# Image-row ConvNeXt kernel: channel sums from PSUM, w1 centered by broadcast transposes, image 0 multiplied before its norm

## The chip, the cores and the metric

The kernel runs on one core of a Trainium2 chip. The metric is the device time of one execution in microseconds; the median of three runs is given. A core has TensorE (PE), VectorE (DVE), ScalarE (ACT), GpSimd (POOL) and the queue SP, which only issues DMAs. Each takes its instructions in order and waits on semaphores for the others.

## The reference

The input is 32 images of 384 channels and 28x28 points, float32. Layer 0 is a ConvNeXt block, layer 1 a gate (only the first concerns us here):

```python
y = conv(x, dw_w, 7x7, padding 3, one filter per channel) + dw_b
mu, var = mean and variance of y over the channels
y = (y - mu) * rsqrt(var + 1e-6) * ln_g + ln_b
y = gelu(y @ w1 + b1)                      # 384 -> 1536
gx = sqrt(sum over the points of y**2); nx = gx / (mean of gx over channels + 1e-6)
y = grn_g * (y * nx) + grn_b + y
x = x + (y @ w2 + b2)                      # 1536 -> 384
# layer 1: per image, mean/max/min of x over the points -> 384 logits; sigmoid(logit + x)
```

## The kernel before

It has two stages under one scheduler, which takes the program in the order it is written and moves an instruction ahead where it counts it as ready; `keep` (keep_in_program_order) pins the order of those it is given.

**Stage 1, convolution of all images.** 48 steps `s` of 8 channels (`TC`), four "pairs" each. In `conv`, a channel takes three matmuls (L639, L641, L643) with a band matrix `tmat` from DRAM as weights and `xt` as the moving side; rows are cut into 7 groups of 4 image rows (`NJ`), so 7 x 32 images = 224 columns. The result `pc` (PSUM, one bank for a pair, 4 banks) is turned by VectorE into `yt` (L646), squared by ScalarE (L651), and the squares of four channels are added to `ssum` by GpSimd (L663). `yt` goes to DRAM `yd` after each step, and `sums_y` (L669) reduces the step's 8 channels to the running channel sum, which is the ninth row of the next `yt`. Beside it, every four steps the next 32 channels of x are loaded, padded (`pad_x`, L452) and turned by TensorE (`turn_x`, L464; copied out of PSUM at L473 or L475).

Also in stage 1 the weights are prepared. w1 is loaded into `ws`; `center_w` forms b1 + w1'ln_b (`pb`, L545), multiplies w1 by ln_g (L551) and takes each column's mean over the channels away, by products with a matrix of -1/C (`pm`, L559, added at L564). With columns that sum to zero, the mean of y need not be taken away before the product. `form_w` makes sums of weight blocks (L530, L533, L536), which go to DRAM as `u1d` and `u2d`: stage 2 multiplies 3x2 and 4x4 blocks with fewer products than blocks, by sums of weight blocks (UPSTEPS, STEPS) and of data blocks (FORMS, SUMS). `U1` and `U2` are the steps at which these begin, `later` holds the step of each weight load.

The last two steps are computed twice, for images 0 to 15 and then 16 to 31, so that the norm of the first half is ready earlier. `finish` makes 1/sqrt(var + eps) of a half (L692 to L699) and stores it as `rsd`. `first_image` spreads the norm's row for image 0 over all partitions by TensorE (`pr`, L729), multiplies the rows of image 0 by it (L736) and makes its ten data forms (`forms_up`, L342) on VectorE.

**Stage 2, image by image.** `up(b)` (L913) does the first product, 15 steps for each of 4 groups of weight tiles, in two halves `t2` = 0 and 2; its PSUM results are copied by ScalarE (L920) or added by VectorE (L922 to L930) into `y`. `gelu` (L883) and `square` (L889) are ScalarE's, `grn` makes the scale of each channel, `scale` (L315, L317) applies it, `sums` (L1002) makes 39 data sums on GpSimd, `down(b)` (L1041) does the second product in 38 steps. `normed(b)` (L308) multiplies the rows of image b, loaded back from `yd`, by its norm `rb`, which comes by DMA from `rsd`; `forms_up(b)` follows on GpSimd. What is done beside the products is written out by hand: `within(b)` and `beside(b)` hang each piece on a step, `(t2, 2 * i + t - t2)` in `up` and `i` in `down`. For image 0, `within(0)` hangs normed(1) and forms_up(1) into `up(0)`, and `within(1)` hangs image 0's second half of gelus, its squares, `grn`, scales and sums into `up(1)`; `down(0)` comes after `up(1)`.

Memory of stage 1's pools (`tp`, `xtp`, `ufp`, `ycp`, `sqp`) is taken again by stage 2's, in order of address: weights, `rb`, `te`, `junk` and the first of `y` lie on `tp`, the rest of `y` and `xp` on `xtp`, `d_room` on the end of `xtp` and what follows it. A new pool's first writer waits until the old pools that it lies on are done with. Before the change the late sums and norms lie in a last `xt` tile (`late_tiles`).

Of the kernel before, what the change touches and what calls it, by code (L numbers as in the profile page):

```python
# [33 lines left out]
TC = 8  # L34
# [163 lines left out]
def convnext_gate_kernel(  # L198
# [75 lines left out]
    def load_y(b):  # L274
        yi = yis[b] = yip.tile([P, CB, NQD, YR], F32, tag="yi", name=f"yi_{b}")
        rb = rbs[b] = rbp.tile([P, NQD, YR], F32, tag="rb", name=f"rb_{b}")

        with tc.issue_after(last_u2[-1]) if last_u2 else ExitStack():
            for cb in range(CB):
                load_y_part(b, yi, cb, 0, P)  # L280
        base = rsd[0 if b < B0 else 1]
        nc.sync.dma_start(
            rb,
            bass.AP(
                tensor=base.tensor,
                offset=base.offset + b * YR,
                ap=[[0, P], [B * YR, NQD], [1, YR]],
            ),
        )
# [29 lines left out]
    def forms_up(b, eng=nc.gpsimd):  # L319

        acc = accs.pop(b)
# [13 lines left out]
        n = 0  # L335
        for name, place, in0, in1, op in FORMS:
            if place and name == "w":
                d = o[place]
            else:
                d = af[n]  # L340
                n += 1
            tc.keep_in_program_order(eng.tensor_tensor(d, o[in0], o[in1], op))  # L342
            o[name] = d


    with ExitStack() as one:
# [5 lines left out]
        psc = one.enter_context(tc.tile_pool(name="psc", bufs=4, space=bass.MemoryType.PSUM))  # L352
        sqp = one.enter_context(tc.tile_pool(name="sqp", bufs=2))

# [69 lines left out]
        ssum = tp.tile([P, SQ, YR], F32, name="ssum")  # L424
        dws = tp.tile([P, 1], F32, name="dws")
        less = tp.tile([P, P], F32, name="less")
        nc.vector.memset(less, -1.0 / C)
# [56 lines left out]
        U1, U2 = 6, 24  # L484
# [38 lines left out]
        def form_w(name, wv, text, dst):  # L523
# [8 lines left out]
            else:  # L532
                nc.gpsimd.tensor_scalar(t, blks[0][1], float(blks[0][0]), None, ALU.mult)  # L533
# [5 lines left out]
        def center_w(part):  # L539

            if part == 0:
                pb = psx.tile([P, 4, P], F32, tag="pt", name="pb").rearrange("p a b -> p (a b)")
                for f in range(FB):
                    for cb in range(CB):
                        nc.tensor.matmul(  # L545
                            pb[:, f : f + 1], w1r[:, cb, f * P : (f + 1) * P],
                            lnb_t[:, cb : cb + 1], start=(cb == 0), stop=(cb == CB - 1),
                        )
                nc.vector.tensor_tensor(b1f, pb[:, :FB], b1_t, ALU.add)
                for cb in range(CB):  # L550
                    nc.vector.tensor_scalar(  # L551
                        w1r[:, cb], w1r[:, cb], lng_t[:, cb : cb + 1], None, ALU.mult
                    )
                return
            f0 = (part - 1) * 4 * P
            pm = psx.tile([P, 4, P], F32, tag="pt", name=f"pm_{part}")
            pm = pm.rearrange("p a b -> p (a b)")
            for cb in range(CB):
                nc.tensor.matmul(  # L559
                    pm, less, w1r[:, cb, f0 : f0 + 4 * P], start=(cb == 0), stop=(cb == CB - 1)  # L560
                )
            for cb in range(CB):
                w = w1r[:, cb, f0 : f0 + 4 * P]
                nc.vector.tensor_tensor(w, w, pm, ALU.add)  # L564
# [12 lines left out]
        for i in range(NG):  # L577
# [20 lines left out]
            3: (  # L598
# [7 lines left out]
            1: (fv, fvec.rearrange("v (fb p) -> p v fb", p=P)),  # L606
            2: (cv, cvec.rearrange("v (cb p) -> p v cb", p=P)),
# [7 lines left out]
        def conv(s, c2, yt, xt, b0, b1):  # L615
# [30 lines left out]
            nc.vector.transpose(yt[:, cy : cy + 2, :], pc[:, :, :N])  # L646
            nonlocal sq
            if cy % SQ == 0:
                sq = sqp.tile([P, SQ, YR], F32, tag="sq", name=f"sq_{cc}_{b0}")
            for ci in range(2):  # L650
                nc.scalar.activation(  # L651
                    sq[:, cy % SQ + ci, :], yt[:, cy + ci, :], AF.Square,
                    bias=dwb[:, cc + ci : cc + ci + 1], scale=1.0,
                )
            if cy % SQ == SQ - 2:
                if cc < SQ:
                    nc.gpsimd.tensor_copy(ssum, sq)
                elif b1 < B:
                    nc.gpsimd.tensor_tensor(
                        late["s2"], ssum if s == NK - 2 and cy < SQ else late["s2"], sq, ALU.add  # L660
                    )
                else:
                    nc.gpsimd.tensor_tensor(ssum, ssum, sq, ALU.add)  # L663
# [3 lines left out]
        def sums_y(dst, yt, n0, n1):  # L667

            nc.vector.tensor_reduce(  # L669
                dst, yt[:, n0:n1, :].rearrange("p c n -> p n c"), AX.X, ALU.add  # L670
            )

        def new_yt(name):
            return ycp.tile([P, TC + 1, YR], F32, tag="yc", name=name)

        late, pcs = {}, []

        def late_tiles():

            t = new_xt(NX).rearrange("p c n -> p (c n)")  # L680
            n = 0
            for name, c in (
                ("yb0", TC + 1), ("yb1", TC + 1), ("s2", SQ), *((f"t{i}", 1) for i in range(10))
            ):
                late[name] = t[:, n * YR : (n + c) * YR].rearrange("p (c n) -> p c n", n=YR)
                n += c

        def finish(yt, part, s2, half):

            s1, s2r, mu, va = (late[f"t{1 + 5 * half + i}"][:, 0] for i in range(4))  # L690
            sums_y(s1, yt, TC - SQ, TC + 1)
            nc.vector.tensor_reduce(s2r, s2.rearrange("p c n -> p n c"), AX.X, ALU.add)  # L692
            nc.vector.scalar_tensor_tensor(mu, s1, dws, part, ALU.add, ALU.add)
            nc.vector.scalar_tensor_tensor(s1, mu, 1.0 / C**2, mu, ALU.mult, ALU.mult)
            nc.vector.scalar_tensor_tensor(va, s2r, 1.0 / C, s1, ALU.mult, ALU.subtract)
            nc.vector.tensor_scalar(va, va, 0.0, EPS, ALU.max, ALU.add)
            nc.scalar.activation(s2r, va, AF.Sqrt)
            rs = s1
            nc.vector.reciprocal(rs, s2r)  # L699
            nc.scalar.dma_start(rsd[half], rs)  # L700
            return rs
# [6 lines left out]
        def spread(k, q, xn):  # L708
            for n in plan[q]:
# [4 lines left out]
                turn_x(i, h, xn)  # L714

        def first_image(n, yt):

            if n == 1:
                firsts["rs"] = finish(yt, firsts["part"], late["s2"], 0)
            elif n == 2 * PAIRS:  # L720
                rs = firsts["rs"]
                pr = [
                    psx.tile([P, 4, P], F32, tag="pt", name=f"pr_{i}").rearrange(
                        "p a b -> p (a b)"
                    )[:, : 2 * YR].rearrange("p (q n) -> p q n", n=YR)
                    for i in range(2)
                ]
                for q in range(NQD):
                    nc.tensor.matmul(  # L729
                        pr[q // 2][:, q % 2], ident[:, q * B : q * B + 1].to_broadcast([P, P]),  # L730
                        rs, start=True, stop=True,
                    )
                accs[0] = room_acc
                for cb in (1, 2, 0):
                    for i in range(2):
                        nc.vector.scalar_tensor_tensor(  # L736
                            room_acc[:, cb, i * NH : (i + 1) * NH].rearrange(
                                "p (r w) -> p r w", w=HW
# [515 lines left out]
```

## Time and profile before

| | us |
|---|---|
| median of 3 runs | 3106.68 (3104.93 to 3108.34) |
| the profiled execution | 3105.7 |
| its span | 3103.9 |
| TensorE busy in the span | 3021.0 (97%) |
| VectorE, ScalarE, GpSimd busy | 2110.7, 1772.9, 2455.4 |

Stage 1 takes the first 541 us, the rest is stage 2, 32 images of which each later one takes the same steps. A matmul of float32 shows as two records in the trace, a transpose as one; 16 records of L639 are one convolution step.

### The profile page before, as it was taken

To read this page: it belongs to the slowest core of one execution; us is meant where nothing else is said; L and a number is where in the kernel's file an instruction comes from. 1 tells how busy PE (TensorE), PEld (TensorE's weight loads), DVE (VectorE), ACT (ScalarE), POOL (GpSimd) and SP (SyncE) were. 2 spreads that over 40 slices of the span, in tenths; PEclk is the share of its full clock that TensorE was granted. 3 is DMA by queue.
4 is the path that set the end of the run, shared out by engine and by line. 5 is a ranking of instruction groups with operands and counts; after the bars stand their busy time and mean duration, and the time that the engine had idled before them with its cause. 6 is when DMAs were issued, how large, how long until landed. Compare 5 with 4: busy or idle time off the path is not lost.

```text
span 3103.9 us, 43870 instructions
## 1 busy us (share of the span) xinstructions
PE 3021.0 (97%) x14437; PEld 2441.4 (79%) x14437; DVE 2110.7 (68%) x4502; ACT 1772.9 (57%) x2886; POOL 2455.4 (79%) x1841
## 2 busy tenths in 40 slices
PE   7999989699999999999999999999999999999998
PEld 7899989377777777777777777777777777777777
DVE  5688778766666666666666666666666666666666
ACT  4354443465666666666666666666666666666662
POOL 3365868279888888888888888888888888888897
PEclk9899999899999999999999999999999999999999
DMA  9799987555666666666666666666666666666646
GB/s 337 260 356 363 330 313 265 155 158 159 198 201 200 202 202 200 201 202 201 200 202 202 201 201 201 201 201 202 202 200 201 202 201 201 202 201 199 196 152 202
DMA packets 287946, 672.77 MB, mean 217 GB/s; under 512 B 31183, under 2 KB 111082, under 8 KB 281706
## 3 DMA queue, kind: packets, MB, share of 16 engines
q1 hardware_dynamic: 274340, 630.94, 61.8%
q10 hardware_dynamic: 13382, 39.03, 3.3%
q8 instruction: 118, 1.93, 0.3%
q14 instruction: 106, 0.87, 0.1%
HBM read 575.11 MB, written 94.76 MB: 216 GB/s over the span
## 4 chain that ended last, share of the span: by engine, by line
PE 86%; DVE 6%; POOL 4%; DMA 2%; issue 1%; ACT 1%; SPq 0%; DVEq 0%; ACTq 0%; POOLq 0%
PE ph_C L913 13%; PE ph_A L913 12%; PE ph_B L913 11%; PE pz_A L1041 8%; PE pz_C L1041 8%; PE pz_F L1041 7%; PE pz_D L1041 7%; PE pc L639 4%; PE pc L641 3%; PE pc L643 3%; PE pz_H L1041 2%; PE pt L464 2%; PE pz_I L1041 2%; PE pz_E L1041 2%; POOL d_room L1002 2%; DVE room L308 2%
## 5 line engine op out<-in xcount | busy, mean ns | idle before, releaser
L317 ACT ACTIVATE y<-y,fv,gsc 128x784 f32<-128x784 f32 x372 | 359.0, 1031 | 469.2 <-DVE gsc L949 469.2
L1002 POOL TENSOR_TENSOR d_room<-y 128x588 f32<-128x588 f32 x253 | 364.6, 1442 | 316.7 <-PE pz_B L1041 192.2
L913 PE MATMUL ph_B<-room,ws 128*128 128x392 f32 x1240 | 461.8, 495 | 12.7 <-ACT y L920 8.5
L913 PE MATMUL ph_C<-room,ws 128*128 128x392 f32 x1240 | 463.4, 496 | 5.2 <-DVE y L926 2.6
L883 ACT ACTIVATE y<-y,b1f 128x784 f32<-128x784 f32 x384 | 350.4, 945 | 206.7 <-DVE y L928 184.0
L913 PE MATMUL ph_A<-room,ws 128*128 128x392 f32 x1240 | 459.0, 492 | 3.0 <-POOL room L342 2.0
L1002 POOL TENSOR_TENSOR d_room<-d_room,y 128x588 f32<-128x588 f32 x308 | 440.8, 1436 | 16.8
L913 PEld LDWEIGHTS ph_C<-room,ws 128*128 128x128 f32 x1240 | 234.3, 191 | 188.9 <-DVE y L926 27.7
L913 PEld LDWEIGHTS ph_B<-room,ws 128*128 128x128 f32 x1240 | 235.8, 191 | 178.1 <-ACT y L920 9.5
L913 PEld LDWEIGHTS ph_A<-room,ws 128*128 128x128 f32 x1240 | 235.7, 190 | 176.3 <-POOL room L342 2.7
L889 ACT ACTIVATE junk<-y 128x784 f32<-128x784 f32 x384 | 329.2, 857 | 9.0
L663 POOL TENSOR_TENSOR ssum<-ssum,sq 128x896 f32<-128x896 f32 x95 | 198.8, 2093 | 167.5 <-ACT sq L651 165.0
L1002 POOL TENSOR_TENSOR d_room<-y,d_room 128x588 f32<-128x588 f32 x214 | 306.0, 1435 | 27.2 <-PE pz_D L1041 15.7
L342 POOL TENSOR_TENSOR room<-room 128x392 f32<-128x392 f32 x300 | 300.4, 1018 | 11.8
L1002 POOL TENSOR_TENSOR y<-y 128x588 f32<-128x588 f32 x180 | 258.7, 1437 | 7.1
L924 DVE TENSOR_TENSOR y<-y,ph_B 128x392 f32<-128x392 f32 x256 | 137.4, 556 | 158.9 <-ACT y L883 127.6
L651 ACT ACTIVATE sq<-yt,dwb 128x224 f32<-128x224 f32 x376 | 152.7, 470 | 158.9 <-DVE yt L646 149.0
L922 DVE TENSOR_TENSOR y<-y,ph_C 128x392 f32<-128x392 f32 x384 | 212.6, 561 | 26.9 <-PE ph_C L913 1.2
L639 PE MATMUL pc<-xt,tmat 128*128 128x224 f32 x736 | 202.9, 358 | 15.4 <-DVE yt L646 7.2
L1041 PE MATMUL pz_A<-d_room,u 128*128 128x196 f32 x1050 | 202.9, 329 | 0.4 <-DMA u<-u2d 0.3
L1041 PEld LDWEIGHTS pz_A<-d_room,u 128*128 128x128 f32 x1050 | 178.8, 190 | 8.1 <-issue 0.6
L641 PE MATMUL pc<-xt,tmat 128*96 128x192 f32 x736 | 181.2, 328 | 0.0
(267 smaller groups left out, 6400.2 us busy)
## 6 DMA issues: line engine op xcount, KB each, us to landing
u<-u2d SPq DMA_DIRECT2D x487, 384.0 KB, 3.7
ws<-u1d SPq DMA_DIRECT2D x384, 320.0 KB, 3.0
tmat<-fs SPq DMA_DIRECT2D x47, 1420.0 KB, 10.0
ws<-u2d SPq DMA_DIRECT2D x121, 384.0 KB, 4.1
yi<-yd SPq DMA_DIRECT2D x95, 448.0 KB, 6.2
yd<-yt SPq DMA_DIRECT2D x46, 896.0 KB, 5.8
x<-in_x SPq DMA_DIRECT2D x32, 1176.0 KB, 5.5
out<-x ACTq DMA_DIRECT2D x31, 1176.0 KB, 9.5
```

The costliest lines, as they stand in the source:

```text
L317: eng.activation(out, in_, AF.Identity, bias=add, scale=mul)
L342: tc.keep_in_program_order(eng.tensor_tensor(d, o[in0], o[in1], op))
L639: keep(nc.tensor.matmul(po, t[:, c, P : 2 * P], xc, start=True, stop=False))
L641: nc.tensor.matmul(lo, t[:, c, 2 * P : T0 + MW], after, start=False, stop=False)
L651: nc.scalar.activation(sq[:, cy % SQ + ci, :], yt[:, cy + ci, :], AF.Square, bias=dwb[:, cc + ci : cc + ci + 1], scale=1.0,)
L663: nc.gpsimd.tensor_tensor(ssum, ssum, sq, ALU.add)
L883: nc.scalar.activation(y, y, AF.Gelu, bias=b1f[:, f : f + 1], scale=1.0)
L889: nc.scalar.activation(junk, ys[b][:, f, :], AF.Square, accum_out=ssqs[b][:, f : f + 1])
L913: nc.tensor.matmul(banks[t, bk][:, :NH], wts[t][:, i % UG, :], o[opnd], start=(first == 1), stop=True, skip_group_check=True,)
L922: nc.vector.tensor_tensor(d, d, p, ALU.add)
L1002: nc.gpsimd.tensor_tensor(d[0], o[a][0], o[c][0], ALU.add if sign == "+" else ALU.subtract)
L1041: nc.tensor.matmul(pz[:, :NQ4], wt[:, i % UD, t, :], o[opnd][0][:, t, :], start=(first and t == 0), stop=(t == KD - 1), skip_group_check=True,
```

## The change

Five things are done.

1. *Channel sums straight from PSUM.* `sums_y` goes. VectorE adds each `pc` to an accumulator `acc` (two channels side by side) right after the transpose, and ScalarE squares `pc` itself instead of `yt`. Sums stay in the layout of `pc`; `finish` adds and reduces them, works on half of the columns and turns the result by one VectorE transpose. `ssum`, `acc`, `fin`, `dws` lie in a new pool `finp` at the end of stage 1's memory; `pc` has 5 banks instead of 4.
2. *Centering of w1 later.* w1 is loaded at step 2 instead of 3 and centered after steps 7 to 9 instead of 4 and 5 (`U1` 10 instead of 6, and three forms in two steps). `pb` takes two columns, ln_b and -ln_g/C, so that its second gives the means `mcol`; twelve products of a broadcast column of `mcol` with the identity spread them over the partitions, and one VectorE instruction multiplies by ln_g and adds.
3. *First terms of weight forms and half of `turn_x`'s copies* go to ScalarE.
4. *Image 0's products are made of its rows without the norm.* `first_image` adds only dw_b to the rows (`raw`), the first two blocks before the half steps, where q, t and u are formed on GpSimd; the other forms follow on VectorE after them, and only then both `finish`. Since the norm is a factor of each point, it is put on after the product: `stretch` multiplies y of image 0 by `rb` before each gelu.
5. `rb` of image 0 lies in `d_room`; normed(1) and forms_up(1) move from steps (0, 18) and (0, 24) to (0, 24) and (2, 0).

The diff, cut:

```diff
+    def load_rb(b):
+        if b == 0:
+            rb = d_room[:, : NQD * YR].rearrange("p (q n) -> p q n", n=YR)
+        else:
+            rb = rbp.tile([P, NQD, YR], F32, tag="rb", name=f"rb_{b}")
+        rbs[b] = rb
...
+        if b in feats:
+            o, af = feats[b], early_af.pop()
+            make_forms(b, eng, o, af, [d for d in FORMS if d[0] not in EARLY])
+            return
...
+        make_forms(b, eng, o, af, [d for d in FORMS if not early or d[0] in EARLY])
+    EARLY, early_af = ("q", "t", "u"), []
...
-        psc = one.enter_context(tc.tile_pool(name="psc", bufs=4, space=bass.MemoryType.PSUM))
+        psc = one.enter_context(tc.tile_pool(name="psc", bufs=5, space=bass.MemoryType.PSUM))
+        finp = one.enter_context(tc.tile_pool(name="finp", bufs=1))
...
-        ssum = tp.tile([P, SQ, YR], F32, name="ssum")
+        ssum = finp.tile([P, SQ, N], F32, name="ssum")
+        acc = finp.tile([P, 2, N], F32, name="acc")
+        fin = finp.tile([P, 3, N], F32, name="fin")
+        for t in (ssum, acc, fin[:, 0]):
+            nc.gpsimd.memset(t, 0.0)
...
-        U1, U2 = 6, 24
+        U1, U2 = 10, 23
...
-                nc.gpsimd.tensor_scalar(t, blks[0][1], float(blks[0][0]), None, ALU.mult)
+                nc.scalar.activation(t, blks[0][1], AF.Identity, scale=float(blks[0][0]))
...
+                nc.vector.tensor_copy(lr[:, :, 0], lnb_t)
+                nc.vector.tensor_scalar(lr[:, :, 1], lng_t, -1.0 / C, None, ALU.mult)
...
-                            pb[:, f : f + 1], w1r[:, cb, f * P : (f + 1) * P],
-                            lnb_t[:, cb : cb + 1], start=(cb == 0), stop=(cb == CB - 1),
+                            pb[:, 2 * f : 2 * f + 2], w1r[:, cb, f * P : (f + 1) * P],
+                            lr[:, cb], start=(cb == 0), stop=(cb == CB - 1),
...
+            for i in range(4):
+                nc.tensor.matmul(
+                    pm[:, i], mcol[:, f0 + i : f0 + i + 1].to_broadcast([P, P]), ident,
+                    start=True, stop=True,
+                )
             for cb in range(CB):
-                nc.tensor.matmul(
-                    pm, less, w1r[:, cb, f0 : f0 + 4 * P], start=(cb == 0), stop=(cb == CB - 1)
-                )
-            for cb in range(CB):
-                w = w1r[:, cb, f0 : f0 + 4 * P]
-                nc.vector.tensor_tensor(w, w, pm, ALU.add)
+                w = w1r[:, cb, f0 * P : (f0 + 4) * P]
+                nc.vector.scalar_tensor_tensor(
+                    w, w, lng_t[:, cb : cb + 1], pm.rearrange("p a b -> p (a b)"),
+                    ALU.mult, ALU.add,
+                )
...
-            nc.vector.transpose(yt[:, cy : cy + 2, :], pc[:, :, :N])
+            keep(nc.vector.transpose(yt[:, cy : cy + 2, :], pc[:, :, :N]))
+            a = part(acc)
+            keep(nc.vector.tensor_tensor(a, a, part(pc[:, :, :N]), ALU.add))
...
-                    sq[:, cy % SQ + ci, :], yt[:, cy + ci, :], AF.Square,
+                    part(sq)[:, cy % SQ + ci], part(pc[:, :, :N])[:, ci], AF.Square,
...
+                nc.gpsimd.tensor_tensor(part(ssum), part(ssum), part(sq), ALU.add)
...
+        def finish(half, b0, b1):
+            rs, s2 = (part(fin[:, i]) for i in range(2))
+            mu, va = (part(acc[:, i]) for i in range(2))
+            keep(nc.vector.tensor_tensor(mu, mu, va, ALU.add))
+            keep(
+                nc.vector.tensor_reduce(
+                    s2,
+                    ssum.rearrange("p c (j b) -> p j b c", b=B)[:, :, b0:b1],
+                    AX.X, ALU.add,
+                )
             )
+            keep(nc.vector.tensor_scalar(mu, mu, dws, 1.0 / C, ALU.add, ALU.mult))
+            keep(nc.vector.tensor_tensor(va, mu, mu, ALU.mult))
+            keep(nc.vector.scalar_tensor_tensor(va, s2, 1.0 / C, va, ALU.mult, ALU.subtract))
+            keep(nc.vector.tensor_scalar(va, va, 0.0, EPS, ALU.max, ALU.add))
+            nc.scalar.activation(s2, va, AF.Sqrt)
+            keep(nc.vector.reciprocal(rs, s2))
+            keep(nc.vector.transpose(fin[:, 2], fin[:, 0]))
+            nc.sync.dma_start(rsd[half], fin[:, 2])
...
-                turn_x(i, h, xn)
+                turn_x(i, h, xn, (nc.vector, nc.scalar)[h])
...
+            if part == 0:
+                raw(nc.scalar, 0, 0, NQD)
+                raw(nc.scalar, 1, 0, NQD)
+                forms_up(0, nc.gpsimd, early=True)
+            else:
+                raw(nc.vector, CB - 1, NQD // 2, NQD)
+                raw(nc.scalar, CB - 1, 0, NQD // 2)
+                forms_up(0, nc.vector)
...
-                first_image(2 * PAIRS, firsts["y"])
+                first_image(1)
+                finish(0, 0, B0)
                 if B0 < B:
-                    finish(y2[1], part, ssum, 1)
+                    finish(1, B0, B)
...
-                yn = new_yt(f"yt_{s + 1}")
-                sums_y(yn[:, TC, :], yt, 0, TC + 1)
-                yt = yn
+                yt = new_yt(f"yt_{s + 1}")
...
-            if U1 - 2 <= s < U1:
-                for part in ((0, 1), (2, 3))[s - U1 + 2]:
+            if U1 - 3 <= s < U1:
+                for part in ((0,), (1,), (2, 3))[s - U1 + 3]:
                     center_w(part)
...
+    def stretch(f, eng):
+        y = ys[0][:, f, :].rearrange("p (r w) -> p r w", w=HW)
+        eng.tensor_tensor(y, y, rows(rbs[0]), ALU.mult)
...
-                at((0, 18), normed, 1)
-                at((0, 24), forms_up, 1)
+                at((0, 24), normed, 1)
+                at((2, 0), forms_up, 1)
+            for m in range(HF):
+                at((2, 4 * m), stretch, m, nc.gpsimd)
...
             for m in range(HF):
+                at((0, 2 * m), stretch, HF + m, (V, nc.gpsimd)[m % 2])
                 at((0, 2 + 2 * m), gelu, p, HF + m)
...
+    load_rb(0)
     if B > 1:
         load_y(1)
```

The load of w1 moves in `later` from step 3 to 2, that of `fvec` from 1 to 4, that of `cvec` from 2 to 1.

## The prediction

> **What bounds the kernel now.** I first read the page's two lines of busy tenths and clock.
>
> ```profile
> PE   7999989699999999999999999999999999999998
> ...
> PEclk9899999899999999999999999999999999999999
> ```
>
> From slice 10 on TensorE is full; the weak slices are the first ten, up to about 700 us, and the diff touches only what is issued there. So I cut that stretch at the stage borders: columns are us, busy time of each engine (instructions), granted clock, DMA share, GB/s.
>
> ```profile
> 19.50:72.30 52.80, 51.69 (x314) 49.32 (x314) 34.61 (x40) 23.61 (x45) 16.30 (x12) 0.97 0.96 335
> 72.30:98.80 26.50, 20.36 (x80) 17.51 (x80) 8.90 (x11) 3.09 (x8) 4.14 (x2) 0.55 0.81 327
> 98.80:114.00 15.20, 15.20 (x78) 12.05 (x77) 11.34 (x15) 5.66 (x11) 4.37 (x3) 1.00 0.38 117
> 114.00:250.00 136.00, 136.00 (x863) 132.04 (x862) 113.18 (x133) 66.64 (x137) 86.32 (x55) 1.00 0.95 335
> 250.00:518.40 268.40, 256.69 (x1588) 245.67 (x1587) 206.27 (x232) 117.44 (x251) 198.55 (x142) 0.99 0.88 325
> 518.40:541.50 23.10, 21.15 (x192) 20.45 (x192) 22.24 (x26) 9.83 (x25) 21.88 (x14) 1.00 0.68 220
> 541.50:577.90 36.40, 9.70 (x20) 5.56 (x20) 27.88 (x35) 5.89 (x16) 6.23 (x3) 0.65 0.40 117
> 577.90:616.10 38.20, 38.19 (x109) 21.89 (x110) 27.16 (x48) 22.68 (x42) 9.98 (x10) 0.93 0.58 187
> 616.10:657.10 41.00, 40.36 (x124) 22.80 (x123) 31.67 (x59) 35.69 (x64) 17.08 (x12) 1.00 0.34 108
> 657.10:701.70 44.60, 41.38 (x231) 39.49 (x230) 21.13 (x69) 20.99 (x30) 43.35 (x33) 0.96 0.70 225
> ```
>
> The convolution runs to 518.4, its two half-batch steps to 541.5; `up(0)` starts in earnest at 577.9, `up(1)` at 616.1, `down(0)` at 657.1. Two stretches have TensorE mostly waiting or at half clock: 72.3 to 98.8 (centering of w1) and 541.5 to 577.9 (first image). Next, what TensorE did in the first, and what it waited for (total us, times, longest).
>
> ```profile
> L545 PE MATMUL pb<-cv,ws 128*128 128x1 f32 x72 | 15.5, 352 | 5.8 <-DMA ws<-in_w 5.8
> L559 PE MATMUL pm<-ws,less 128*128 128x512 f32 x18 | 10.3, 728 | 0.3 <-DVE ws L551 0.3
> ```
>
> ```profile
> PE pr L729 <- DVE xt L699: 13.1, 1, 13.1
> PE ph_B L913 <- ACT y L920: 8.5, 1, 8.5
> PE pc L639 <- DVE yt L646: 7.2, 2, 4.7
> PE ph_B L913 <- DVE room L342: 4.2, 1, 4.2
> ```
>
> The first image waits for its norm (L699, the reciprocal), the forms (L342), and then for ScalarE, which the waits over all engines trace to memory:
>
> ```profile
> ACT y L920 <- DMA rsd<-xt: 8.1, 1, 8.1
> ```
>
> y doesn't read rsd; its memory lies where the first stage's tiles lay. Last, the chain of waits from 627 on:
>
> ```profile
> 627.17 1.28 ACT L937
> ...
> 641.37 1.76 POOL d_room L1002
> ...
> 644.93 5.63 POOL d_room L1002 x4
> ```
>
> From 641.37 GpSimd's sums (L1002) run without a hole until 697, then forms for image 2 until 707. TensorE loses only 7 us over `down(0)` (44.6 us for 38 steps of 0.995), but it is paced by GpSimd: what counts at the end is when the sums start, 641.4, not when `up(0)` does.
>
> [...] 0.55 in 72.3:98.8, and the 72 passes of L545 take 15.49/72 = 215 ns. [...] So these passes should take 107 ns at full clock (estimate); the transposes of L464, three in 0.33 us in the chain, show that rate. [...]
>
> **The change, part by part.** Times are against the profiled execution (3105.7 us, span 3103.9; median of the runs 3106.7, so 1 us more).
>
> *Centering.* Before: w1 arrives 5.8 us late, 72 passes take 15.5, three pm matmuls 5.0 at half clock, six more 5.15: with 0.3 of wait, 31.8 us. After: w1 is asked for at step 2 and used after step 7, so no wait. The 72 passes stay (two columns for one): 7.7 us at full clock. The 9 pm matmuls of 512 columns become 12 of 128, two passes each: 24 x 107 ns = 2.6. Sum 10.3 at full clock. Bounds: L545 at half clock did not bring the clock back in 15 us, so such thin matmuls may also lose it; then half of the passes at 215 ns and some convolution at half clock, 16. I take 13.5: gain 18. VectorE's lng multiplies and 9 additions become 9 fused instructions of about 0.7 us; hidden, as TensorE goes on with the convolution.
>
> *Convolution steps.* TensorE starts of steps are 39.06 us apart per four undisturbed steps, 9.765 a step (last two, without transposes, 8.23). From step 20 to 46 the 26 steps take 268.5 us where the matmuls need 24 x 9.765 + 2 x 8.23 = 250.8: 17.7 lost. The cause named is VectorE's transpose L646, held up by the 3.7 us reduction L669. VectorE per step before: 4 x 0.633 + 3.71 + 2 x (0.667 + 0.535) = 8.64 of 9.77 us. After: no reduction, four additions from PSUM (392 columns take 0.56, so 448 some 0.62), and half the copies go to ScalarE: 4 x 0.633 + 4 x 0.62 + 2 x 0.667 = 6.35, none longer than 0.7. ScalarE: 8 x 0.47 + 2 x 0.853 + 2 x 0.49 + some 0.5 for the first terms of weight forms = 6.9. Squares from PSUM are not in the trace; bounds 0.35 (L920 reads 392 in 0.50) to 0.5 us, not decisive. GpSimd loses 28 first terms of 1.2 to 1.5 us. The moved loads of cv and fv, the three GpSimd memsets at the start (before the first x has come) and the later u1 forms (three in two steps, under GpSimd's load) I put at nothing. Of the 17.7 I give back 14 (bounds 8 to 17). Added wait: a pc bank is now freed by VectorE and by ScalarE's squares, which wait for sq buffers that GpSimd frees, and behind them stand ScalarE's copies for the next k; five banks instead of four, about 12 us, cover this.
>
> *Half steps.* A channel takes 0.63 us, 32 make 20.2; before 23.1, with 2.7 of waits at start. After 21: gain 2. VectorE per pair 0.63 + 0.35, under TensorE's 1.26.
>
> So the convolution ends at T = 541.5 - 18 - 14 - 2 = 507.5.
>
> *First image.* Before, from 541.5: norm 13.1, pr and room, forms, L920's wait. After, T + 1.3 last VectorE addition, T + 1.9 raw rows of the last block, T + 2.6 form p, and 7 forms in 4.5 us feed TensorE. The eight `pr` passes are gone; q, t, u are made on GpSimd during the half steps (3 x 1.02, hidden). y now lies on `tp` and `xtp` alone; `fin` and `ssum` lie in `finp`, under d_room, so L920 needn't wait for rsd. Late next: the two finishes, about 3.5 us each on VectorE (reduction 0.9, reciprocal of half the columns 0.8, small ones 0.25, a wait for ScalarE's square root), placed after the forms. Behind them on VectorE stand the PSUM additions of `up(0)`; TensorE then waits for a bank: 0 to 7 us, I take 3.5. `up(0)` starts at T + 3, ends at T + 46, not at conv end + 74.6 (616.1).
>
> *Stretch, and what then is late.* rb is needed for image 1 and now image 0: store of rsd after T + 9.8 (6.2 us to land), load of rb (5.7): T + 22; rb(0) goes into d_room, after both stores, T + 25. SP's queue carries both with the u1 loads of the second half behind; 320 KB take 3 us, so at worst a few us. normed(1) 3 us, forms_up(1) on GpSimd 10 x 1.02: until T + 35. Then six multiplications by rb of 784 columns on GpSimd, 2.0 us each (392 take 1.02), until T + 47, three more in `up(1)` until T + 53; three on VectorE (1 us). Each gelu of image 0 waits for its multiplication; behind it on ScalarE stand L920's PSUM copies, for which TensorE waits. ScalarE's first gelu is at T + 37.5; 12 gelus (0.87 apart), 12 squares (0.98) and 14 copies (0.43) are 28 us: T + 65.5. Before, the square root came at 627.17 and the continuous sums 14.2 us later; after, sums start at T + 80 (bounds T + 73 to T + 88). Before they started 641.4 - 541.5 = 99.9 after convolution end. So of the 31 us won at the start of `up(0)` 20 remain.
>
> Sum: 18 + 14 + 2 + 20 = 54; 3105.7 - 54 = 3051.7, about 3053 as a median. From `up(2)` on nothing is touched: TensorE is busy 2381 of 2398 us there.
>
> **Rivals.**
> A, the forecast: 3053, chance 0.6, with 3040 to 3068 from the bounds above.
> B, the stretch becomes the wait: ScalarE's copies stand behind gelus that wait for GpSimd, and TensorE of `up(0)` and `up(1)` with them. For: GpSimd is given 10.2 + 12 us in a half of `up` that TensorE does in 19.7. Against: 8 banks and the order of issue may let copies pass first. Sums then at T + 98: 54 - 18 = 36 gained, 3071. Chance 0.18.
> C, the sums hardly slip (stretches ahead of forms_up, thin matmuls at full clock): 20 + 10 and 21 instead of 18: 67 gained, 3040 or just below. Chance 0.12.
> D, slower: the convolution is paced by the banks. ScalarE's squares hold pc until GpSimd frees sq; GpSimd was busy 198.6 of 268.4 us in the late convolution. The 20 us at the end are used up when the steps average 11.0 us instead of 9.7 ((541.5 + 20 - 21 - 1 - 19.5 - 13.5)/46), as 10.85 was the average with all stalls before. At 11.5 it costs 46 x 0.5 = 23: 3130. Against: 6.9 us of ScalarE's work in 9.77. Chance 0.07.
> E, no change within 0.2% (6 us, what a measurement of this kernel can tell from none): B and part of D together, 3106, chance 0.03.
>
> **How the numbers follow.** Faster 0.6 + 0.18 + 0.12 = 0.90, less a little for an unknown wait, 0.88; same 0.03; slower 0.09. The range 3038 to 3084 holds A, C's upper part and B with its bound; left out are D, E and the tail of C.
>
> **What would show it.** Right: L545's 72 passes in 8 to 12 us with no wait ahead; VectorE some 65% busy in 114:250; step starts near 9.8 apart after step 20; a hole of 3 to 5 us between pc_half and ph_B; first continuous sums near 587. Wrong: TensorE's pc waits for ACT sq; holes over 10 us in `up(0)` before L920's copies; a late rb(0) that moves the gelus.

## The result and the profile after

The changed kernel takes 3079.22 us (median of 4 runs, 3078.53 to 3081.39); the kernel before, beside it, 3106.09. The ratio is 0.9914 with a 95% interval of 0.9897 to 0.9931: faster by 27 us, where 53 was forecast. The profiled execution has a span of 3079.6 us.

The busy tenths and the clock on the page of the kernel after:

```profile
PE   8999999899999999999999999999999999999998
...
PEclk9899999999999999999999999999999999999999
```

The weak slices have become fewer and milder; besides the first, one is left, at 540 to 616 us. Cut at the same borders as before (us, then busy time and number of instructions of PE, PEld, DVE, ACT, POOL, granted clock, DMA share, GB/s), after:

```profile
...
240.40:501.70 261.30, 253.18 (x1590) 244.13 (x1589) 147.14 (x262) 141.39 (x327) 184.23 (x128) 1.00 0.91 337
501.70:525.50 23.80, 22.07 (x193) 21.74 (x192) 14.99 (x34) 9.62 (x33) 17.80 (x17) 0.93 0.68 207
525.50:550.00 24.50, 22.37 (x62) 12.16 (x63) 21.75 (x46) 8.37 (x18) 1.98 (x2) 0.93 0.77 217
550.00:590.00 40.00, 27.94 (x67) 14.79 (x66) 17.59 (x31) 16.69 (x30) 24.61 (x18) 0.83 0.53 173
590.00:631.00 41.00, 38.67 (x117) 21.08 (x116) 34.77 (x61) 36.16 (x64) 19.77 (x14) 1.00 0.29 95
631.00:675.60 44.60, 40.23 (x231) 37.73 (x230) 21.92 (x69) 21.03 (x30) 43.34 (x33) 1.00 0.69 223
675.60:3076.00 2400.40, 2383.01 (x10794) 1867.74 (x10792) 1598.13 (x3824) 1456.03 (x2252) 2038.43 (x1537) 1.00 0.61 197
```

Read it from the borders. Step 20 of the convolution starts at 240.4 instead of 249.9 (9.5 won), step 46 at 501.7 instead of 518.4 (7.2 more), the convolution ends at 525.5 instead of 541.5 (0.7 lost in the half steps): 16.0 us up to here, where 34 was forecast. `up(0)` starts at 527.6, and the 40 us from 550, `up(0)`'s second half, hold only 27.9 us of TensorE at a clock of 0.83. `down(0)` begins at 631.0 instead of 657.1. From there on next to nothing has changed: TensorE is busy 2383 of 2400 us, before 2381 of 2398.

What TensorE waited for until 700 us:

```profile
PE pc L661 <- ACT sq L681: 10.1, 7, 2.7
...
PE ph_A L914 <- ACT te L921: 4.9, 1, 4.9
PE ph_A L914 <- ACT y L921: 3.9, 2, 3.6
PE ph_B L914 <- ACT y L921: 3.5, 1, 3.5
```

All four name ScalarE. The first are new stalls in the convolution, of 1.7 to 2.7 us at steps 5, 23, 39 and 40 and three of 0.3. The other three are holes in `up(0)`. What ScalarE itself was doing at the first of those holes (start, duration, instruction, idle time ahead of it), and GpSimd beside it:

```profile
555.86 0.95 ACT L879 ACTIVATE y<-y,b1f 128x784 f32<-128x784 f32 x1 [11.04 <-POOL y L884]
556.72 0.86 ACT L921 ACTIVATE y<-ph_B 128x392 f32<-128x392 f32 x2
...
562.37 0.95 ACT L879 ACTIVATE y<-y,b1f 128x784 f32<-128x784 f32 x1 [4.01 <-POOL y L884]
563.23 0.86 ACT L921 ACTIVATE y<-ph_A 128x392 f32<-128x392 f32 x2
```

```profile
554.00 1.83 POOL L884 TENSOR_TENSOR y<-y,d_room 128x784 f32<-128x784 f32 x1 [25.15 <-PE ph_A L914]
555.79 1.99 POOL L356 TENSOR_TENSOR d_room<-acc 128x392 f32<-128x392 f32 x2
557.73 1.85 POOL L884 TENSOR_TENSOR y<-y,d_room 128x784 f32<-128x784 f32 x1
559.53 1.01 POOL L356 TENSOR_TENSOR d_room<-d_room,acc 128x392 f32<-128x392 f32 x1
```

A gelu (L879) stands at the head of ScalarE's queue for 11.0 us, until GpSimd's first stretch (L884) is done; right behind it are two PSUM copies (L921) whose data had been ready, and TensorE resumes 0.5 us after the first of them has begun. Each further stretch waits its turn among the forms of image 1 (L356). `rb(0)`, which the first stretch reads, landed at 553.4, 28 us after the convolution's end instead of 25; this is what GpSimd's 25.15 us of idle time ended with, though the view names a TensorE instruction for them. So it looks as rival B was drawn.

Last, the centering, in the lines of TensorE from 96 to 145 us, and three stretches with their clock:

```profile
L566 PE MATMUL pb<-lr,ws 128*128 128x2 f32 x72 | 13.0, 318 | 0.0
L577 PE MATMUL pm<-ident,mcol 128*128 128x128 f32 x24 | 3.3, 279 | 0.0
```

```profile
96.70:108.20 11.50, 11.50 (x81) 11.25 (x79) 7.96 (x15) 7.31 (x18) 6.26 (x3) 1.00 1.01 408
108.40:121.80 13.40, 13.40 (x59) 13.07 (x59) 0.25 (x2) 0.00 (x0) 0.00 (x0) 0.50 0.81 311
121.90:143.50 21.60, 21.58 (x147) 20.86 (x146) 15.09 (x28) 11.74 (x28) 8.36 (x5) 1.00 0.55 189
```

TensorE never waits, yet at 108.3, 2.6 us after the first of the 72 thin passes, its clock falls to half and stays there for 13.7 us. The first 24 passes took 2.6 us, the other 48 took 10.4.

Three explanations were tried, one for each place: thin passes halve the clock; a gelu waiting for its stretch holds the copies behind it; and, for the convolution, either the banks held by ScalarE, or the store of `yt`, or the order of VectorE's queue.

### The profile page after: what moved, and what is told of

Read it like the earlier page. It is cut to its first block, busy times and chain, and to the rows that moved or that the text cites. A ratio compares the mean times of both kernels' runs of the same rounds, so it can differ in the third digit from the quotient of the medians.

```text
span 3079.6 us, 44014 instructions
## 1 busy us (share of the span) xinstructions
PE 3013.7 (98%) x14435; PEld 2437.3 (79%) x14435; DVE 1985.0 (64%) x4555; ACT 1802.5 (59%) x3004; POOL 2438.4 (79%) x1829
## 3 DMA queue, kind: packets, MB, share of 16 engines
q1 hardware_dynamic: 275156, 631.62, 62.4%
## 4 chain that ended last, share of the span: by engine, by line
PE 87%; POOL 7%; DVE 3%; issue 1%; ACT 1%; DMA 1%; ACTq 0%; SPq 0%; DVEq 0%; POOLq 0%
PE ph_C L914 13%; PE ph_A L914 12%; PE ph_B L914 11%; PE pz_A L1042 7%; PE pz_C L1042 7%; PE pz_D L1042 7%; PE pz_F L1042 6%; PE pc L661 5%; PE pc L663 4%; PE pc L665 4%; POOL d_room L1003 3%; PE pt L483 2%; PE pz_H L1042 2%; PE pz_E L1042 2%; PE pz_I L1042 2%; DVE room L315 2%
## 5 line engine op out<-in xcount | busy, mean ns | idle before, releaser
L879 ACT ACTIVATE y<-y,b1f 128x784 f32<-128x784 f32 x384 | 350.1, 945 | 230.5 <-DVE y L929 180.2
L686 POOL TENSOR_TENSOR ssum<-ssum,sq 128x896 f32<-128x896 f32 (+1 forms) x100 | 201.7, 2017 | 150.6 <-ACT sq L681 148.7
L356 POOL TENSOR_TENSOR room<-room 128x392 f32<-128x392 f32 x303 | 303.5, 1018 | 11.9
L661 PE MATMUL pc<-xt,tmat 128*128 128x224 f32 x736 | 203.5, 358 | 15.4 <-ACT sq L681 10.1
L665 PE MATMUL pc<-xt,tmat 128*128 128x192 f32 x736 | 181.2, 328 | 0.0
## 6 DMA issues: line engine op xcount, KB each, us to landing
tmat<-fs SPq DMA_DIRECT2D x47, 1420.0 KB, 10.5
```

Source lines behind the costliest of these rows:

```text
L661: keep(nc.tensor.matmul(po, t[:, c, P : 2 * P], xc, start=True, stop=False))
L665: keep(nc.tensor.matmul(hi, t[:, c, :P], before, start=False, stop=True))
L686: nc.gpsimd.tensor_tensor(part(ssum), part(ssum), part(sq), ALU.add)
L879: nc.scalar.activation(y, y, AF.Gelu, bias=b1f[:, f : f + 1], scale=1.0)
```

## The experiments

Times of all kernels, and where they stand: T is the end of the half steps, sums the start of the continuous data sums on GpSimd (the point that the prediction took for the end).

| kernel | median, us | ratio, 95% | steps 20 to 46 | T | sums, after T |
|---|---|---|---|---|---|
| before | 3106.1 | | 268.5 | 541.5 | 99.9 |
| the change | 3079.2 | 0.9897-0.9931 | 261.3 | 525.5 | 89.8 |
| the change again | 3078.9 | 0.9902-0.9929 | 263.0 | 523.1 | 90.6 |
| thin passes in thirds | 3074.2 | 0.9884-0.9911 | 263.0 | 519.6 | 88.8 |
| gelus behind copies | 3066.5 | 0.9861-0.9891 | 263.0 | 523.9 | 76.8 |
| yt in halves | 3080.6 | 0.9906-0.9931 | 265.1 | 522.9 | 92.1 |
| squares from yt | 3075.2 | 0.9887-0.9914 | 257.3 | 513.3 | 93.2 |
| copies kept | 3067.5 | 0.9861-0.9888 | 252.5 | 510.7 | 89.5 |
| before, copies kept | 3092.2 | 0.9949-0.9976 | 251.3 | 538.4 | 86.8 |
| three together | 3051.0 | 0.9810-0.9837 | 253.3 | 509.0 | 76.8 |
| and stretches shared | 3051.3 | 0.9809-0.9836 | 252.4 | 506.4 | 77.5 |
| and thin in sixths | 3046.4 | 0.9794-0.9821 | 252.4 | 506.3 | 77.9 |

Each ratio is to the kernel before, run beside it on the same chip. The change again and the three below it shared one chip; squares from yt, copies kept, three together and stretches shared had a second, the last two experiments a chip each. The kernel before took 3104.9 to 3107.0 us on them, so a difference across chips is good to some 2 us.

**The change again.** The same kernel, on the chip of the next three.

> The changed kernel once more, beside the others on one chip, as the level from which they are read. Every theory expects 3079 us within 3 us; in its profile the stretch from the end of the half-batch steps (525.5) to the first of the continuous sums (615.3) is again about 90 us.

It came out at 3078.88 us (3075.20 to 3082.99).

**Thin passes in thirds.** The passes of `pb` are issued in three lots of 24, after steps 5, 6 and 7, with a convolution step between them, and kept in program order:

```diff
-            if U1 - 3 <= s < U1:
-                for part in ((0,), (1,), (2, 3))[s - U1 + 3]:
+            if U1 - 5 <= s < U1:
+                for part in ((0,), (-1,), (-2,), (1,), (2, 3))[s - U1 + 5]:
...
-                for f in range(FB):
+                for f in range(4):
```

> The 72 thin passes (two columns) are done in three lots of 24 after steps 5, 6 and 7 instead of in one run of 72 after step 7. [...] a lot of 24 takes 2.6 us, less than the time after which the clock halved inside the run of 72 (24 passes at 0.11 us, then 48 at 0.21), so all 72 stay at 0.11 us: 5.1 us less for them and some 1.8 us less for the convolution behind them that ran at half clock; kernel 5 to 8 us faster than the changed one, about 3072. Rival, the passes are slow by themselves (weight loads that nothing hides): their sum stays at 13 us and the time at 3079 within 2.

3074.17 us, 4.7 less than the change beside it. In the trace the granted clock was 0.95 on average from 70 to 136.6 us, in that of the change 0.87. That makes some 7 us at half clock of the 66.6 instead of 17 (an estimate from the two averages). In the three together, whose lots are the same, 24 passes took 2.6 to 2.7 us, 0.11 a pass, as the first 24 of the change did; the time above that came with the half clock.

**Gelus behind the copies.** The six gelus of image 0's first half are hung at later steps of `up(0)` and kept in program order, behind ScalarE's last PSUM copies:

```diff
-        nc.scalar.activation(y, y, AF.Gelu, bias=b1f[:, f : f + 1], scale=1.0)
+        a = nc.scalar.activation(y, y, AF.Gelu, bias=b1f[:, f : f + 1], scale=1.0)
+        if pin:
+            tc.keep_in_program_order(a)
...
-                at((2, 2 + 4 * m), gelu, b, m)
+                at((2, 2 + 4 * m if b else min(20 + 2 * m, 28)), gelu, b, m, b == 0)
```

> The first six gelus of image 0 are pinned behind ScalarE's last PSUM copy of up(0); nothing else is moved. Theory queue: TensorE's holes in up(0) of 3.5, 3.6 and 4.9 us and the half clock after them come from copies that stand behind gelus which wait for GpSimd's multiplications; they go, up(0) ends some 15 us sooner, its last rows are multiplied sooner, and the sums start 8 to 11 us sooner: about 3070. Rival GpSimd: the multiplications and the forms of image 1 (21 us of GpSimd's work from 554 on) set the gelus whatever stands before them; the sums start within 3 us of where they did, 3077 to 3080, though the holes are gone.

3066.51 us, 12.4 less. The waits of all engines from 545 to 590 us in this run:

```profile
...
ACT y L879 <- POOL y L886: 5.0, 2, 4.3
PE ph_A L916 <- POOL d_room L356: 5.0, 1, 5.0
```

The gelus (L879) now wait 5.0 us in all, where in the kernel after they waited 27.5 and the first alone 11.0. Of TensorE's waits for ScalarE's copies 1.3 us are left; `up(1)` starts at 567.2 instead of 586.1 in the change again. What is late next is GpSimd: the first block of `up(1)` waits 5.0 us for a form of image 1. The sums start at T + 76.8, so of the 19 us won at the start of `up(1)` 13 arrive.

**yt in halves.** VectorE's transposes sometimes wait for the store of a former `yt` (DMA yd<-yt). Here each turned tile is two, stored after two pairs, so that it comes free earlier:

```diff
-        ycp = one.enter_context(tc.tile_pool(name="ycp", bufs=2))
+        ycp = one.enter_context(tc.tile_pool(name="ycp", bufs=4))
...
-            return ycp.tile([P, TC, YR], F32, tag="yc", name=name)
+            return [ycp.tile([P, SQ, YR], F32, tag="yc", name=f"{name}_{h}") for h in range(2)]
```

> The turned tile that goes to DRAM is cut in two of four channels (four buffers of half the size, two stores a step, in the last two steps eight). Theory store: the convolution's waits before L661 (10 us, named ScalarE's squares, which wait for VectorE's additions, which stand behind a transpose that waits for the store of the tile two steps back, 9 us to land) go, since a buffer comes free half a step sooner: steps 20 to 46 take 254 instead of 261 us, kernel 5 to 8 us faster, about 3073. Rival squares: ScalarE's part in holding the PSUM banks is the cause; steps 20 to 46 stay at 261 within 2, kernel at 3079 or slower by the added DMA issues in the last steps.

3080.64 us; the stalls at steps 23, 39 and 40 stayed and steps 20 to 46 took 265.1. The store isn't what TensorE waits for. But the timeline of VectorE around step 23 showed what is (the change again, 266 to 272 us; the last line is TensorE's stall there):

```profile
266.46 0.69 DVE L492 COPY xt<-pt 128x512 f32<-128x512 f32 x1 [4.19 <-PE pt L483]
271.34 0.69 DVE L492 COPY xt<-pt 128x512 f32<-128x512 f32 x1 [4.19 <-PE pt L483]
271.94 0.64 DVE L668 STREAM_TRANSPOSE yt<-pc 128x448 f32<-128x448 f32 x1
```

```profile
274.02 1.12 PE L661 MATMUL pc<-xt,tmat 128*128 128x224 f32 x2 [2.73 <-ACT sq L681]
```

From 262.3 to 271.9 VectorE does nothing but two copies of `turn_x` (L492), and waits 4.19 us ahead of each, though TensorE has filled bank after bank. `conv` keeps its transposes and additions in program order, but the copies are not kept, so the scheduler put those of the next tile ahead of the pc transposes (L668) in VectorE's queue. Each copy waits for TensorE's transposes (L483), which TensorE does only after the convolution of the pairs written before them. When the five banks are full, TensorE waits, and it is named after ScalarE because the squares come last.

**Squares from yt.** If ScalarE's hold on the banks were the cause, freeing them without it should end the stalls:

```diff
-                    part(sq)[:, cy % SQ + ci], part(pc[:, :, :N])[:, ci], AF.Square,
+                    sq[:, cy % SQ + ci, :], yt[:, cy + ci, :], AF.Square,
```

> The squares are taken from the turned tile yt again, as before the change, and the sums of squares so belong to wrong points (the norm is wrong, the work the same); a pc bank is then freed by VectorE's addition alone, not by ScalarE. Theory 'ScalarE holds the banks' (the trace names ACT sq as the last releaser at steps 5, 23, 39, 40): those stalls of 2 to 4 us each go, steps 20 to 46 take 252 to 256 us instead of 263, the kernel 3068 to 3073. Theory 'VectorE's queue' (the copies of turn_x are issued ahead of the pc transposes and wait 4 us for TensorE's own transposes): the stalls stay, now named after VectorE; steps 20 to 46 within 2 us of 263, the kernel within 4 us of 3079.

3075.21 us, and 257.3 us for steps 20 to 46: between the two expectations. The stall at step 5 is gone; those at steps 23, 39 and 40 are there, now named after VectorE's additions; step 23 takes 11.1 us instead of 13.6 (undisturbed 9.0), step 39 11.1 instead of 12.0, step 40 as long as before. In sum about half of the loss is left. So ScalarE lengthens a stall that it doesn't begin. Why the squares come late shows in the waits of the change again, where ACT sq <- DVE acc stands with 3.9 us from 262 to 284: the square waits for the addition that reads the same `pc`, and began 0.03 to 0.1 us after its end at each of four pairs from 273 to 277 us. Of the 10 us that T came earlier here, 4 arrived; `up(0)` began at T + 5.4 instead of T + 2.1, since TensorE waited 5.4 us instead of 2.1 for the forms that VectorE makes of image 0. In the half steps the stalls went wholly: they took 20.2 us instead of 22.2.

**Copies kept.** VectorE's copies of `turn_x` are pinned where they are written, and nothing else:

```diff
-                eng.tensor_copy(dst, src)
+                keep(eng.tensor_copy(dst, src))
```

> VectorE's copies of turn_x (L492) are kept in program order, behind the transposes and additions of the pair after which they are written; nothing else is touched. Theory 'VectorE's queue': the stalls at steps 5, 23, 39 and 40 go, steps 20 to 46 take 252 to 256 us instead of 263, the kernel is 7 to 12 us faster than the change as it stands (3067 to 3072). Theory 'ScalarE or GpSimd holds the banks': within 3 us of 3079, waits for ACT sq as before.

3067.49 us, 11.4 below the change again. Steps 20 to 46 take 252.5 us, and the half steps 21.5 instead of 22.2 (23.8 in the first profile of the change). VectorE's groups over these steps, first the change, then with the copies kept (busy us, mean ns | idle time before):

```profile
L668 DVE STREAM_TRANSPOSE yt<-pc 128x448 f32<-128x448 f32 x104 | 66.4, 638 | 28.7 <-PE pc L665 23.5 <-DMA yd<-yt 5.2
...
L492 DVE COPY xt<-pt 128x512 f32<-128x512 f32 x48 | 33.0, 688 | 85.9 <-PE pt L483 85.8
```

```profile
L668 DVE STREAM_TRANSPOSE yt<-pc 128x448 f32<-128x448 f32 x104 | 67.2, 646 | 104.7 <-PE pc L665 60.6 <-DMA yd<-yt 35.9 <-PE pt L483 8.1
...
L492 DVE COPY xt<-pt 128x512 f32<-128x512 f32 x48 | 32.5, 677 | 0.0
```

The idle time hasn't gone; it has moved from the copies (85.9 us to none) to the transposes (28.7 to 104.7), even the wait for the store is seven times as long, and yet TensorE takes 1.7 us more than the 250.8 that its matmuls need, instead of 10.5. An engine that is ahead may wait; what hurt here was a wait at the head of its queue for something that TensorE does later than what stands behind it.

**Before, copies kept.** The prediction had put the 17.7 us that these steps lost before the change down to the reduction L669. Here the kernel before keeps its reductions, and its copies and transposes are pinned:

```diff
-            nc.vector.transpose(yt[:, cy : cy + 2, :], pc[:, :, :N])
+            keep(nc.vector.transpose(yt[:, cy : cy + 2, :], pc[:, :, :N]))
...
-                eng.tensor_copy(dst, src)
+                keep(eng.tensor_copy(dst, src))
```

> The kernel before, with VectorE's transposes L646 and its copies of turn_x (L473) kept in program order; the reductions L669 stay. It tells what the 17.7 us were that steps 20 to 46 lost before the change. Theory 'the reduction holds the transposes' (the prediction's): the loss stays, steps 20 to 46 within 3 us of 268.5, the time within 3 us of before. Theory 'the order of VectorE's queue was the loss there too': steps 20 to 46 take 253 to 258 us and the kernel before is 8 to 14 us faster, 3092 to 3098.

Steps 20 to 46, in that kernel's windows and in its VectorE groups:

```profile
247.80:499.10 251.30, 251.30 (x1589) 243.83 (x1589) 207.80 (x235) 121.95 (x253) 199.21 (x143) 1.00 0.94 349
```

```profile
L669 DVE TENSOR_REDUCE yt<-yt 128x224 f32<-128x2016 f32 x26 | 96.8, 3725 | 9.7 <-DMA yd<-yt 8.3 <-ACT sq L651 0.9
```

All 26 reductions are there, 3.7 us each, and TensorE is busy in every one of the 251.3 us: 0.5 above the 250.8 that the matmuls need. With the order pinned the reduction costs the convolution nothing. The kernel is 12.9 us faster than before beside it, by the medians. Not all of the 17 us arrive: the half steps take 39.3 us instead of 23.1 with this pin, one wait of 7.8 (pc_half <- DVE yt_a) among it, and part of that comes back, since the norm is then earlier and the sums start at T + 86.8.

**Three together.** Thin passes in thirds, gelus behind copies and copies kept, in one kernel.

> The thin matmuls in thirds, the first six gelus behind ScalarE's last copy of up(0), and VectorE's copies of turn_x kept, together. If the three places are independent, gains add: 4.7 + 12.4 + what the copies bring (0 or 7 to 12) off 3079: 3062 without, 3050 to 3055 with. If GpSimd's order (sums of image 0 behind forms_up(1)) is what ends last, the earlier convolution still shifts it whole, so no other number.

3050.98 us. The three gains, 4.7 + 12.4 + 11.4 = 28.5 off 3078.9, give 3050.4: they add. Run once more beside the last experiment, it gave 3051.26 (3046.53 to 3054.36).

> The e6 kernel again, beside it on the same chip: 3049 to 3053.

**Stretches shared.** As the three together, and every other of the first six stretches on VectorE:

```diff
-                at((2, 4 * m), stretch, m, nc.gpsimd)
+                at((2, 4 * m), stretch, m, (nc.gpsimd, V)[m % 2])
```

> As e6, and every other of the first six stretches on VectorE instead of GpSimd. Theory 'GpSimd's turn of stretches and forms is what up(1) waits for': the 5 us wait of ph_A for d_room at the start of up(1) goes, the second wait for the stretched y too, and 3 to 6 us more than e6. Rival 'VectorE's additions of up(0) stand behind stretches that wait for rb': new holes in up(0), same or slower than e6.

3051.30 us: the same. The wait for image 1's forms, 2.1 us in the three together, went, but `ph_C` then waited 2.2 us for a VectorE addition, and the sums start at T + 77.5. The 3 to 6 us didn't come. Of GpSimd's ten forms of image 1 four took some 1.7 us here, and three in the three together, where in the change again all took 1.0 (the last section has more on VectorE's stretches).

**Thin passes in sixths.** As the three together, with six lots of 12 passes, two in each of steps 5 to 7:

```diff
+                    if U1 - 5 <= s < U1 - 2 and c2 % 2:
+                        center_w(-2 * (s - U1 + 5) - c2 // 2)
...
-                for f in range(4):
+                for f in range(2):
```

> As e6, with the 72 thin passes in six lots of 12 (1.3 us each), two in each of steps 5 to 7, instead of three lots of 24. In e6 each lot of 24 was followed by 3.4 us at half clock, and steps 5 to 9 took 65.8 us (49.15 without centering). Theory [...] no half clock at steps 5 to 9, which take 60 to 62 us, and the kernel is 3 to 6 us faster than e6. Rival [...] as many us at half clock as in e6 (10) or more, same time or slower.

3046.40 us (3044.83 to 3050.16), 4.9 below the run beside it, though their ranges overlap. The trace has one stretch of half clock instead of three, and 62.4 us for steps 5 to 9 instead of 65.8. The first three lots and what came before them:

```profile
77.99 1.40 PE L568 MATMUL pb<-lr,ws 128*128 128x2 f32 x12
85.29 1.50 PE L568 MATMUL pb<-lr,ws 128*128 128x2 f32 x12 [0.58 <-ACT xt L494]
93.28 1.40 PE L568 MATMUL pb<-lr,ws 128*128 128x2 f32 x12
```

Of all six only the second, with 0.58 us of idle ahead of it, was followed by half clock (87.7 to 91.1). This trace alone doesn't show that sixths are better than thirds: its execution took 3050.16 us, within the range of the run beside it. What speaks for sixths is the mean granted clock of each run: 0.998 in four of the five and 0.996 in the profiled one, where none of the 13 runs with thirds and the two other repairs was above 0.996. Where the rest of the half clock went in those four can't be seen, as they have no trace. This is the fastest of the versions: 0.9808 of before (0.9794 to 0.9821), and its interval lies below that of the change.

## Why the prediction was right, and where it was wrong

Faster, and within the range, but by half of the size. That the range held is in part luck: its upper end, 3084, was drawn for rival B with its bound, and B came together with a loss in the convolution that the text had not seen. Its sum was 18 + 14 + 2 + 20 = 54; measured, in the same terms, 9.5 + 7.2 - 0.7 + 10.1 = 26.1.

*Centering, 18.* The stretch fell from 31.8 to 17.5 us, not 13.5. The mechanism was in the text as the upper bound: half of the passes at 215 ns and some convolution at half clock, 16; in fact two thirds of the passes ran at half clock. The likelier value should have been the bound, since the trace of before already showed 72 such passes with the clock at 0.50 for all of their 15.5 us. The 107 ns a pass at full clock were the author's estimate, and the first 24 passes took that, 2.6 us; what failed was the assumption that the clock would stay: in the other 10.4 us of thin passes it was at 0.50. The thin passes in thirds, 4.7 us faster with less half clock, agree that the clock made the difference. Of the 14.3 us won here 9.5 were left at step 20. Some things put at nothing weren't: the first step began 1.35 us later and took 1.0 longer (ScalarE's last copies ahead of it came at 19.9 us instead of 18.6, and half clock lasted 6.8 us there instead of 3.4; which edit did it is open), and step 5 took 14.0 instead of 10.1 us (the queue stall again, and its half clock); against these, step 3 lost 1.4 less.

*Convolution steps, 14.* This is the step that failed, in its reason and not only its size: "the cause named is VectorE's transpose L646, held up by the 3.7 us reduction L669". The first half is what the trace said; the second was added because the reduction was the longest instruction in VectorE's queue. The kernel before with its copies kept shows that the reduction costs TensorE nothing there. What held the transposes was the copies that the scheduler had put ahead, 49.3 us of waits for TensorE's own transposes (DVE xt L473 <- PE pt L464, steps 20 to 46). The change left that order possible, so 10.5 of the 17.7 us stayed. VectorE's work was priced well: additions from PSUM 0.58 us against 0.62.

*Half steps, 2.* None came, and here rival D was at work on a small scale. The chain in the profile of the change, ScalarE's wait and then TensorE's:

```profile
516.69 0.35 ACT L681 ACTIVATE sq<-pc_half,dwb 128x112 f32<-128x112 f32 x1 [4.12 <-POOL ssum L686]
```

```profile
517.34 0.47 PE L661 MATMUL pc_half<-xt,tmat 128*128 128x112 f32 x2 [1.72 <-ACT sq L681]
```

A square waits for an sq buffer that GpSimd frees late, as the three early forms of image 0, which the text called hidden, stand ahead of its additions; TensorE waits for the square, and 3.4 us of half clock follow. With squares from yt ScalarE waited nearly as long for GpSimd (6.2 us in all instead of 7.0), but held no bank, and the half steps took 20.2 us, what their matmuls need. With the copies kept they took 21.5, with 0.8 us of that wait left.

*First image.* `up(0)` was to start at T + 3 and started at T + 2.1. The 31 us that the text counts as won at this start are 33 by its own times (36.4 less 3); the 20 that remain follow from the sums and don't rest on them.

*Stretch and sums, 20.* The sums started at T + 89.8, outside the bounds of T + 73 to 88. Rival B, with a chance of 0.18, named the mechanism word for word, and its price was T + 98. The argument against it, that the order of issue may let copies pass first, was not looked into, and it is just what didn't hold: `up(1)` started at T + 62 instead of T + 46. With the gelus moved behind the copies the sums start at T + 76.8, inside the forecast's bounds. The holes were 3.5 to 4.9 us and not over 10, but with the second and third came 6.8 us of half clock each, which neither case had priced.

*Rival D.* Its sign appeared, TensorE waiting for ACT sq, 10.1 us. In steps 20 to 46 its mechanism, the sq buffers that GpSimd frees, isn't the cause: ScalarE waited 0.7 us for them there, and squares from yt show ScalarE's part as a lengthening. In the half steps it is.

The version with all three repairs takes 3051 us with T at 509.0, where the text had 3053 and 507.5: what was forecast was there to be had, behind three losses of which the text had one as a bound, one as a rival, and missed one.

## What to carry to other kernels

When a wait names an instruction, look at what stood ahead of it in its queue and what that was waiting for, before blaming the longest instruction nearby: here an order of issue cost more than 26 reductions of 3.7 us. Pinning some instructions of an engine lets the scheduler move the unpinned ones past them, so pin those too that wait for work issued later. Work put into a stage should go behind the copies that free TensorE's banks (12.4 us here), and thin matmuls among thick ones (4.7 us here in three lots).

## What the runs showed of the hardware

Matmuls that move 2 columns kept TensorE busy without a hole, yet after 2.6 us of them the granted clock fell to 0.50, and 10.4 us more of them didn't bring it back. Up to 700 us the trace of the change has eight stretches of half clock, of 3.4 to 13.7 us, and that of before six, of 3.4 to 23.9; each was 3.4 us or a multiple of it, to within 0.1 us. In the three together each of the three lots of 24 passes (2.6 to 2.7 us) was followed by half clock, with convolution matmuls of 0.84 us instead of 0.49, and the clock was 0.91 on average from 70 to 130 us; of the six lots of 12 (1.4 us) one was, and the average was 0.97. What decides when the clock falls isn't shown: of the three holes in `up(0)`, those of 3.6 and 4.9 us came with half clock and that of 3.5 us without.

A stretch of 784 columns took 1.85 us on GpSimd while VectorE ran none. On VectorE, which the prediction put at 1 us, it took 2.0 on average (three of them, 1.2 to 2.6), while GpSimd ran the same kind. Each of the three ended 0.8 us after the GpSimd stretch that was running when it began, and GpSimd's second and third took 2.6 us instead of 1.85. So in this trace the stretches handed to VectorE came with slower ones on GpSimd too; by what, it doesn't show.
